# A transformer block on one core: projections two batches further ahead, reciprocals issued between the values' transfers

## The chip, the core and the metric

The kernel runs on one core of a Trainium2 chip. Five engines work side by side, each through its own list of instructions in order: TensorE (PE, matrix products; its weight loads are shown apart as PEld), VectorE (DVE), ScalarE (ACT), GpSimd (POOL) and SyncE (SP), which here issues nearly all transfers. They wait for one another through semaphores. Matmul results stand in PSUM, everything else on chip in SBUF. The metric is the device time of one launch in microseconds (us). An engine that is idle costs nothing unless the work that ends last waits for it.

## What is computed

A batch of 16 sequences, 256 positions of 256 features each, all in float32, goes through one block:

```
x = x + attention(layernorm(x))       # 16 heads of 16 features
x = x + ffn(layernorm(x))             # 256 -> 1024 -> 256
attention: softmax(q @ k.T / 4, keys up to 16 positions ahead) @ v, then @ wo.T
ffn:       silu(h @ gate.T) * (h @ up.T), then @ down.T
```

`gate`, `up` and `down` are not inputs. Each is 1024 x 256 values of a cubic (Catmull-Rom) interpolation of 2033 control points, so the kernel has to make the three matrices before the first feed-forward.

## The kernel before

**Tiling.** A batch is a tile of 128 partitions by 2 x 256. Q and K are kept transposed in `qks`, four heads to a group `g`, each head in its own 32 partitions: 16 features and, for the query, a row with the negated maximum of its scores, so that the exponent is the product itself. `vs` holds V with a column of ones, whose product is the softmax's denominator. Both are rings of NQK = 3 buffers; batch b uses number b % 3. A buffer's constant rows are set once by POOL (`scores_and_values`, L162).

**Steps.** A loop of B + 4 = 20 steps (L596) is a software pipeline. Step s works on five batches at once:

- `pb = s`: `project_qk` (L233: four matmuls each for q and k, two ACT copies into `qkc`, eight transfers into `qks`) and `project_v` (L257); ahead of them, for batch s + 1, `stats_a`, `norm_a` and `turn_a` (mean and variance, normalised rows, transposition through PE and an ACT copy `xnT`).
- `nb = s - 1`: scores for the maxima. `inner` (L318, four per step) and `outer` (L348, two) compute blocks of scores on PE; `find_max` reads them on DVE. `turn_max` (L382) transposes the maxima (`pm`), and four transfers put them into `qks`.
- `tb = s - 2`: the scores again, now with the maximum's row, the exponentials on ACT, their masking on POOL, and `values` for two groups (`po`, copied by ACT into `au`). Maxima and exponentials of one `inner` or `outer` share two PSUM tiles of scores, and the next block of scores waits until both have read.
- `ob = s - 3`: the other half of `values`, then `gather` (L412): four transfers of denominators (`den`) and eight of values, from `au` into `ac`. `invert` (L428) takes the reciprocal on DVE, writes it to memory (`rd`) and reads it back spread over the heads' features (`rb`, two transfers). `divide`, `project_o` (`py`), the sum with x, `stats_f`, `norm_f`, `turn_f` (`ptf`, copied into `x2T`) follow in the same step.
- `s - 4`: the feed-forward. `gate_up` (L471) part i makes 256 of the 1024 intermediate rows, `down` (L493) the output rows, half by half; `out` is stored when the second is done. Part 0 is made a step earlier: at the end of step s, for batch s - 3.

**What sets the order.** `InOrder` (L78) keeps each engine's instructions in program order; the tile framework sees to the waits and buffers. So the order of the calls in the loop (L596 to L635) is the order of work on each engine. Between the attention's pieces lie seven numbered gaps; `fill(s, gap)` (L567) puts the feed-forward of an older batch there, so that PE has work while DVE and ACT read the scores. In steps s >= B, where nothing is projected, the parts of `gate_up` and `down` stand one gap earlier.

Steps 0 to 3 have no feed-forward yet. There the table `heads` (L554) puts into a gap some splines, which make the three matrices (`spline`, L520: four matmuls `pw`, two ACT copies, two predicated DVE copies), and a number of unused products: `keep_running(n)` multiplies the identity with itself n times into a PSUM tile that nothing reads (`run`). Their number over all gaps is 67, after 12 ahead of the first step.

```
heads = {
    (0, 7): (0, 5),
    (1, 1): (1, 3), (1, 3): (1, 9), (1, 4): (0, 6), (1, 5): (1, 3), (1, 6): (0, 4), (1, 7): (0, 11),
    (2, 1): (1, 0), (2, 3): (1, 2), (2, 5): (1, 0), (2, 6): (0, 2), (2, 7): (0, 11),
    (3, 3): (0, 7), (3, 6): (0, 4),
}   # (step, gap): (splines, unused products)
```

**Buffers.** `xs`, the batches' rows, have nine buffers, since a batch's rows are needed from `stats_a` to the output. `au`, `inter`, `qkc` and `xnT` have two each. Two PSUM banks (`ps_m`) serve all products of the attention but the scores, in turn.

Of the kernel before, what the change touches and what calls it, by code (L numbers as in the profile page):

```python
# [11 lines left out]
F32 = mybir.dt.float32  # L12
# [6 lines left out]
P = 128  # L19
B, S, DIM = 16, 256, 256  # L20
H, HD = 16, 16
G = 4
# [71 lines left out]
def block_kernel(  # L94
# [13 lines left out]
    pe, dve, act, pool, sp = (  # L108
        InOrder(tc, e) for e in (nc.tensor, nc.vector, nc.scalar, nc.gpsimd, nc.sync)
    )  # L110
# [3 lines left out]
    sb1 = ctx.enter_context(tc.tile_pool(name="sb1", bufs=1))  # L114
    sb4 = ctx.enter_context(tc.tile_pool(name="sb4", bufs=4))
    sb6 = ctx.enter_context(tc.tile_pool(name="sb6", bufs=6))
    sbx = ctx.enter_context(tc.tile_pool(name="sbx", bufs=9))
    dr = ctx.enter_context(tc.tile_pool(name="dr", bufs=2, space=bass.MemoryType.DRAM))
    ps_s = ctx.enter_context(tc.tile_pool(name="ps_s", bufs=1, space=PSUM))
    ps_f = ctx.enter_context(tc.tile_pool(name="ps_f", bufs=2, space=PSUM))  # L120
# [5 lines left out]
    def load_x(b, engine):  # L126
        xs[b] = sbx.tile([P, 2, DIM], F32, tag="x", name=f"x{b}")
        engine.dma_start(xs[b], x[b].rearrange("(c p) d -> p c d", p=P))

    load_x(0, sp)  # L130
    w_in = {}
    for nm, src in (("q", wqT), ("k", wkT), ("v", wvT), ("o", woT)):
# [8 lines left out]
    for w in range(3):  # L141
        sp.dma_start(cp_in[:, w, :], cps[w])
        if w == 0:
            sp.dma_start(second_in, second)
    load_x(2, sp)


    ident = const.tile([P, P], F32, tag="ident", name="ident")
# [3 lines left out]
    mask0 = const.tile([P, JB], F32, tag="mask0", name="mask0")  # L152
    mask1 = const.tile([P, S], F32, tag="mask1", name="mask1")
    masks = (mask0, mask1)
    NQK = 3
    qks = [
        const.tile([P, 2, G, S], F32, tag=f"qk{i}", name=f"qk{i}") for i in range(NQK)
    ]
# [3 lines left out]
    def scores_and_values(i):  # L162


        pool.memset(qks[i][:, 1], -1.0)

        pool.memset(vs[i], 0.0)
        pool.memset(vs[i][:, :, :, HD : HD + 1], 1.0)
# [13 lines left out]


    xns, xnTs, mxs, aus, aos, recs, x2s, x2Ts = ({} for _ in range(8))
    es, inters, pgs = {}, {}, {}

    moments = {}

# [42 lines left out]
        transposed(xns.pop(b), xnTs[b], f"ta{b}")  # L231

    def project_qk(b):  # L233
        qkc = sb.tile([P, 2, 2, S], F32, tag="qkc", name=f"qkc{b}")
        for i, nm in enumerate("qk"):
            pq = ps_m.tile([P, 2, S], F32, tag="m", name=f"p{nm}{b}")
            for oc in range(2):
                for kc in range(2):
                    pe.matmul(
                        pq[:, oc, :],  # L240
                        lhsT=w_in[nm][:, kc, oc * P : (oc + 1) * P],
                        rhs=xnTs[b][:, kc, :],
                        start=(kc == 0),
                        stop=(kc == 1),
                    )
            act.activation(
                qkc[:, i], pq, AF.Copy, scale=HD**-0.5 if nm == "q" else 1.0
            )
        for gg in range(2):
            for r in range(4):  # L250
                at = 64 * gg + 16 * r

                (act if b == 0 and r % 2 else sp).dma_start(
                    qks[b % NQK][32 * r : 32 * r + HD, :, gg::2, :], qkc[at : at + HD]
                )
# [136 lines left out]

    def values(b, g2):
        if g2 == 0:
            aus[b] = sb.tile([P, G, S], F32, tag="au", name=f"au{b}")
        po = ps_m.tile([P, 2, S], F32, tag="m", name=f"po{b}_{g2}")
        for gg in range(2):
            g = 2 * g2 + gg
            for c, i, n in ((0, 0, S), (1, I1, W1)):
                for r in range(4):  # L400
                    pe.matmul(
                        po[32 * r : 32 * r + 32, gg, i : i + n],
                        lhsT=vs[b % NQK][:, c, 4 * g + r, :],
                        rhs=es[b, 1, g2, r // 2][:, r % 2, gg, :]
                        if c
                        else es[b, 0, g, r // 2][:, r % 2, :],
                        start=(c == 0),
                        stop=(c == 1),
                    )
        act.copy(aus[b][:, 2 * g2 : 2 * g2 + 2, :], po)  # L410

    def gather(b):  # L412

        au = aus.pop(b)
        den = sb.tile([4 * H, 64], F32, tag="den", name=f"den{b}")
        for g in range(G):
            sp.dma_start(
                den[16 * g : 16 * g + 16, :],
                au[HD:P:32, g, :].rearrange("r (q c) -> r q c", q=4),
            )  # L420
        recs[b] = den
        aos[b] = sb.tile([P, 2, S], F32, tag="ac", name=f"ac{b}")
        for gg in range(2):
            for r in range(4):
                at = 64 * gg + 16 * r
                sp.dma_start(aos[b][at : at + HD], au[32 * r : 32 * r + HD, gg::2, :])

    def invert(b):  # L428
        den = recs.pop(b)
        rec = sb.tile([4 * H, 64], F32, tag="rec", name=f"rec{b}")  # L430
        dve.reciprocal(rec, den)
        rd = dr.tile([H, S], F32, tag="rd", name=f"rd{b}")
        sp.dma_start(rd.rearrange("h (q c) -> (h q) c", q=4), rec)
        rb = sb.tile([P, 2, S], F32, tag="rb", name=f"rb{b}")
        for oc in range(2):
            sp.dma_start(
                rb[:, oc, :],
                rd[8 * oc : 8 * oc + 8, :].unsqueeze(1).to_broadcast([8, HD, S]),
            )
        recs[b] = rb  # L440
# [29 lines left out]

    def gate_up(b, i):  # L471
        if i == 0:
            inters[b] = sb.tile([P, 8, S], F32, tag="inter", name=f"inter{b}")
        pp = []
        for nm, w in (("g", gateT), ("u", upT)):
            t = ps_f.tile([P, 2, S], F32, tag="f", name=f"p{nm}{b}_{i}")
            for ic in range(2):
                for kc in range(2):
                    at = (2 * i + ic) * P
                    pe.matmul(  # L480
                        t[:, ic, :],
                        lhsT=w[:, kc, at : at + P],
                        rhs=x2Ts[b][:, kc, :],
                        start=(kc == 0),
                        stop=(kc == 1),
                    )
            pp.append(t)
        th = sb.tile([P, 2, S], F32, tag="th", name=f"th{b}_{i}")
        act.activation(th, pp[0], AF.Tanh, scale=0.5)
        dve.scalar_tensor_tensor(th, th, 1.0, pp[0], ALU.add, ALU.mult)  # L490
        dve.tensor_tensor(inters[b][:, 2 * i : 2 * i + 2, :], th, pp[1], ALU.mult)
# [21 lines left out]
    def coefficients(w):  # L513

        dve.scalar_tensor_tensor(
            cp_in[:, w, :], cp_in[:, w, :], 0.5 if w == 2 else 1.0, tab_in[:, 0:NPART],
            ALU.mult, ALU.mult,
        )
# [28 lines left out]
    def do(stage, b, *args):  # L547
        if 0 <= b < B:
            stage(b, *args)
# [2 lines left out]


    heads = {  # L554
        (0, 7): (0, 5),
        (1, 1): (1, 3), (1, 3): (1, 9), (1, 4): (0, 6), (1, 5): (1, 3), (1, 6): (0, 4), (1, 7): (0, 11),
        (2, 1): (1, 0), (2, 3): (1, 2), (2, 5): (1, 0), (2, 6): (0, 2), (2, 7): (0, 11),
        (3, 3): (0, 7), (3, 6): (0, 4),
    }
    parts = iter([(w, part) for part in range(2) for w in range(2)] + [(2, 0), (2, 1)])  # L560

# [5 lines left out]
    def fill(s, gap):  # L567

        n, idle = heads.get((s, gap), (0, 0))
        if idle:  # L570
            keep_running(idle)
        for _ in range(n):
            spline(*next(parts))

        late = s >= B
        for what, at in (
            ((gate_up, s - 4, 1), 1),
            ((gate_up, s - 4, 2), 2 if late else 3),
            ((gate_up, s - 4, 3), 3 if late else 4),
            ((down, s - 4, 0), 4 if late else 5),  # L580
            ((down, s - 4, 1), 5 if late else 6),
            ((gate_up, s - 3, 0), 7),
        ):
            if at == gap:
                do(*what)


    for t in tiles:
# [5 lines left out]
    norm_a(0)  # L594
    turn_a(0)
    for s in range(B + 4):  # L596
        pb, nb, tb, ob = s, s - 1, s - 2, s - 3
        if 3 <= s + 2 < B:
            load_x(s + 2, sp)
        inner(nb, tb, 0)  # L600
        do(values, ob, 1)
        do(gather, ob)
        if s == 1:
            coefficients(2)
        do(stats_a, pb + 1)
        if s == 0:
            for i in range(1, NQK):
                scores_and_values(i)
        fill(s, 1)
        do(norm_a, pb + 1)  # L610
        if s == 0:
            coefficients(0)
            coefficients(1)
        inner(nb, tb, 1)
        do(invert, ob)
        do(project_qk, pb)
        fill(s, 2)
        outer(nb, tb, 0)
        fill(s, 3)
        inner(nb, tb, 2)  # L620
        do(values, tb, 0)
        do(turn_a, pb + 1)
        do(divide, ob)
        fill(s, 4)
        inner(nb, tb, 3)
        do(project_o, ob)
        do(stats_f, ob)
        fill(s, 5)
        do(norm_f, ob)
        outer(nb, tb, 1)  # L630
        fill(s, 6)
        do(turn_f, ob)
        do(project_v, pb)
        do(turn_max, nb)
        fill(s, 7)  # L635


# [27 lines left out]
```

## Time and profile before

| what | value |
|---|---|
| median of three runs | 680.85 us (678.76 to 681.75) |
| the profiled execution | 683.28 us, its span 681.6 us |
| mean granted TensorE clock | 0.990 |
| PE, scores | 4096 matmuls, 106.4 us busy |
| PE, `pg`, `pu`, `pd` | 127.3, 121.5 and 117.0 us |
| PE, `run` | 158 matmuls, 22.1 us |
| DVE, maxima | 512 of 362 ns, and 512 reads of 83 ns |
| ACT, exponentials | 192 of 615 ns |
| transfers | 29.65 MB, 44 GB/s on average |

The profile comes from one execution, so sums against it are made with its own 681.6 us of span. The span runs from the first to the last instruction; 1.7 us of the execution lie around it. A float32 matmul appears as two records, so 79 unused products are 158 records; transposes appear as one. Where a row of the timeline merges several instructions, it gives the start of the first, the time from there to the end of the last, and how many; brackets hold the engine's idle time before it and what released it. "SPq" rows are transfers being issued, not carried. The ends of matmuls are modelled; the distance from the start of one group to the start of the next is the safer measure of what a group takes.

### The profile page before, as it was taken

The numbers are of one execution on the slowest core, as the hardware profiler recorded it, in microseconds if no ns is written. First come the engines' busy times: TensorE is split into PE (matmuls) and PEld (weight loads), VectorE is DVE, ScalarE is ACT, GpSimd is POOL, SyncE is SP. The second block draws the span as 40 slices with busy tenths as digits, with TensorE's granted clock in tenths as the row PEclk, the third lists the DMA queues.
The fourth block names the chain that finished last, engine by engine and source line by source line (L and its number), as shares of the span: only waits on it lengthen the run. The fifth ranks groups of instructions, "written<-read, shape, count | busy, mean of one in ns | idle before, by whom it ended". The sixth has DMA issues, their size and how long they took to land.

```text
span 681.6 us, 18745 instructions
## 1 busy us (share of the span) xinstructions
PE 661.8 (97%) x7534; PEld 520.9 (76%) x7534; DVE 358.0 (53%) x1473; ACT 230.0 (34%) x413; POOL 124.1 (18%) x244
## 2 busy tenths in 40 slices
PE   7999899999999999999999999999999999999998
PEld 6676677878777787877778787877778787676876
DVE  5656555465464546466454546556554546523332
ACT  2245434243333424243333424333342423232110
POOL 5012211122121212122111112211121111212000
PEclk9999989999999999999999999999999999999989
DMA  7302303021121313012121302112030301010100
GB/s 218 54 17 51 64 21 65 17 67 17 50 49 40 59 33 63 21 43 40 48 51 35 64 18 64 21 50 48 25 59 19 58 24 36 16 27 27 33 15 15
DMA packets 34422, 29.65 MB, mean 44 GB/s; under 512 B 7840, under 2 KB 33696, under 8 KB 34336
## 3 DMA queue, kind: packets, MB, share of 16 engines
q1 hardware_dynamic: 32928, 27.15, 18.0%
q10 hardware_dynamic: 1408, 1.31, 0.7%
q8 instruction: 59, 0.97, 0.6%
q14 instruction: 27, 0.22, 0.1%
HBM read 10.88 MB, written 4.46 MB: 23 GB/s over the span
## 4 chain that ended last, share of the span: by engine, by line
PE 87%; DVE 1%; ACT 0%; issue 0%; POOL 0%; DVEq 0%
PE pg L88 18%; PE pd L88 17%; PE pu L88 16%; PE scores L88 12%; PE po L88 7%; PE py L88 5%; PE pv L88 3%; PE pq L88 3%; PE pk L88 3%; PE ptf L88 1%; PE pta L88 1%; PE pm L88 1%; DVE z L88 0%; ACT e L88 0%; DVE x L88 0%
## 5 line engine op out<-in xcount | busy, mean ns | idle before, releaser
L88 ACT ACTIVATE e<-scores 128x512 f32<-128x512 f32 (+1 forms) x192 | 117.5, 615 | 266.2 <-PE scores L88 206.2
L88 DVE CUSTOM_DVE_ANT_0 z<-scores,mask 128x144 bf16<-128x144 f32 (+1 forms) x512 | 154.5, 362 | 73.8 <-ACT qkc L88 35.5
L88 POOL TENSOR_SCALAR_AFFINE_SELECT e<-e 128x224 f32<-128x224 f32 (+1 forms) x192 | 94.3, 492 | 448.4 <-ACT e L88 448.1
L88 PE MATMUL pg<-x2T,gateT 128*128 128x256 f32 x512 | 127.3, 392 | 1.4 <-ACT x2T L88 1.4
L88 PE MATMUL pu<-x2T,upT 128*128 128x256 f32 x512 | 121.5, 380 | 0.0
L88 DVE SCALAR_TENSOR_TENSOR th<-th,pg 128x512 f32<-128x512 f32 x64 | 44.0, 687 | 140.5 <-ACT th L88 140.5
L88 PE MATMUL pd<-downT,inter 128*128 128x256 f32 x512 | 117.0, 382 | 0.0
L88 PE MATMUL scores<-qk 17*64 17x144 f32 (+7 forms) x4096 | 106.4, 317 | 3.9 <-ACT e L88 1.8
L88 PEld LDWEIGHTS pg<-x2T,gateT 128*128 128x128 f32 x512 | 94.1, 193 | 19.0 <-DVE mx L88 3.1
L88 PEld LDWEIGHTS pu<-x2T,upT 128*128 128x128 f32 x512 | 97.9, 191 | 13.5
L88 PEld LDWEIGHTS pd<-downT,inter 128*128 128x128 f32 x512 | 96.1, 190 | 14.1 <-DVE mx L88 0.2
L88 PEld LDWEIGHTS scores<-qk 17*64 17x64 f32 (+1 forms) x4096 | 69.2, 131 | 40.0 <-issue 30.1
L88 ACT ACTIVATE th<-pg 128x512 f32<-128x512 f32 x64 | 38.2, 597 | 72.2 <-PE pg L88 72.0
L88 DVE TENSOR_TENSOR inter<-th,pu 128x512 f32<-128x512 f32 x64 | 44.0, 688 | 26.6 <-PE pu L88 26.6
L88 PE MATMUL po<-e,v 128*32 128x256 f32 (+1 forms) x1024 | 50.0, 336 | 0.0
L88 PEld LDWEIGHTS po<-e,v 128*32 128x32 f32 x1024 | 29.5, 109 | 23.3 <-issue 12.3
L88 DVE DVE_READ_ACCUMULATOR2_ANT mx<- 128x1 f32 x512 | 42.4, 83 | 0.1
L88 DVE TENSOR_TENSOR x<-x,pd 128x256 f32<-128x256 f32 x32 | 13.5, 421 | 51.5 <-PE pd L88 51.5
L88 PE MATMUL py<-wo,ac 128*128 128x256 f32 x128 | 33.3, 405 | 2.4 <-issue 2.4
L88 PE MATMUL pq<-xnT,wq 128*128 128x256 f32 x128 | 31.9, 392 | 1.1 <-ACT xnT L88 0.7
L88 PEld LDWEIGHTS py<-wo,ac 128*128 128x128 f32 x128 | 23.9, 196 | 11.0 <-issue 7.0
L88 PE MATMUL pv<-wv,xnT 128*128 128x256 f32 x128 | 31.5, 391 | 0.0
(54 smaller groups left out, 421.7 us busy)
## 6 DMA issues: line engine op xcount, KB each, us to landing
qk<-qkc SPq DMA_DIRECT2D x124, 64.0 KB
x<-x SPq DMA_DIRECT2D x16, 256.0 KB
ac<-au SPq DMA_DIRECT2D x128, 32.0 KB
rb<-rd SPq DMA_DIRECT2D x32, 128.0 KB
out<-x SPq DMA_DIRECT2D x15, 256.0 KB
qk<-mxT SPq DMA_DIRECT2D x64, 4.0 KB
den<-au SPq DMA_DIRECT2D x64, 4.0 KB
cp_in<-cps SPq DMA_DIRECT2D x3, 256.0 KB
```

What stands on the lines that cost most here:

```text
L88: return self.tc.keep_in_program_order(fn(*args, **kwargs))
```

## The change

Projections run two batches further ahead (`AHEAD = 2`). In step s from 4 on, batch s + 2 is projected, and batch s + 3 has its statistics, norm and transposition. The two batches that this takes are made up for in steps 1 to 3: a table `projections` says for steps 0 to 3 what is prepared or projected in which gap, and `heads` has other numbers of unused products and two splines in other gaps. Steps 14 and 15 project nothing.

The rings `qks` and `vs` get five buffers, x gets ten; `au` and `inter` get one each, where they had two. `project_qk` is cut in two: the products and copies, and `spread`, the eight transfers, which can come later. A batch's load comes four steps ahead, after `invert` in place of the step's start; the third load now comes before the table `second`, and a fourth after the control points.

Of the eight transfers of values, `gather` issues four; the other four follow the store of the reciprocals in `invert`. `norm_a` stands after `inner(1)` and `invert`, no longer ahead of them. In `fill`, the earlier places of `gate_up` now begin at step 14; those of `down` begin at step 17 (`alone`), no longer at 16.

```diff
-    sbx = ctx.enter_context(tc.tile_pool(name="sbx", bufs=9))
+    sbx = ctx.enter_context(tc.tile_pool(name="sbx", bufs=10))
...
+    AHEAD = 2
     load_x(0, sp)
...
         if w == 0:
+            load_x(2, sp)
             sp.dma_start(second_in, second)
-    load_x(2, sp)
+    load_x(3, sp)
...
-    NQK = 3
+    NQK = 3 + AHEAD
...
     def project_qk(b):
-        qkc = sb.tile([P, 2, 2, S], F32, tag="qkc", name=f"qkc{b}")
+        qkcs[b] = qkc = sb.tile([P, 2, 2, S], F32, tag="qkc", name=f"qkc{b}")
...
+    def spread(b):
+        qkc = qkcs.pop(b)
         for gg in range(2):
...
-            aus[b] = sb.tile([P, G, S], F32, tag="au", name=f"au{b}")
+            aus[b] = sb1.tile([P, G, S], F32, tag="au", name=f"au{b}")
...
-        for gg in range(2):
-            for r in range(4):
-                at = 64 * gg + 16 * r
-                sp.dma_start(aos[b][at : at + HD], au[32 * r : 32 * r + HD, gg::2, :])
+        gather_heads(b, 0)
+
+    def gather_heads(b, gg):
+        for r in range(4):
+            at = 64 * gg + 16 * r
+            sp.dma_start(aos[b][at : at + HD], aus[b][32 * r : 32 * r + HD, gg::2, :])
...
         sp.dma_start(rd.rearrange("h (q c) -> (h q) c", q=4), rec)
+        gather_heads(b, 1)
+        del aus[b]
...
-            inters[b] = sb.tile([P, 8, S], F32, tag="inter", name=f"inter{b}")
+            inters[b] = sb1.tile([P, 8, S], F32, tag="inter", name=f"inter{b}")
...
     heads = {
-        (0, 7): (0, 5),
-        (1, 1): (1, 3), (1, 3): (1, 9), (1, 4): (0, 6), (1, 5): (1, 3), (1, 6): (0, 4), (1, 7): (0, 11),
-        (2, 1): (1, 0), (2, 3): (1, 2), (2, 5): (1, 0), (2, 6): (0, 2), (2, 7): (0, 11),
-        (3, 3): (0, 7), (3, 6): (0, 4),
+        (0, 7): (0, 6),
+        (1, 1): (1, 0), (1, 4): (1, 2), (1, 5): (1, 2), (1, 6): (0, 5), (1, 7): (0, 5),
+        (2, 1): (1, 0), (2, 3): (1, 6), (2, 5): (1, 1), (2, 6): (0, 4),
+        (3, 3): (0, 5), (3, 6): (0, 6),
     }
...
-        late = s >= B
+        alone = s > B
+        late = s >= B - AHEAD
         for what, at in (
             ((gate_up, s - 4, 1), 1),
             ((gate_up, s - 4, 2), 2 if late else 3),
             ((gate_up, s - 4, 3), 3 if late else 4),
-            ((down, s - 4, 0), 4 if late else 5),
-            ((down, s - 4, 1), 5 if late else 6),
+            ((down, s - 4, 0), 4 if alone else 5),
+            ((down, s - 4, 1), 5 if alone else 6),
...
+    projections = {
+        (0, 1): ((stats_a, 1),),
+        (0, 2): (
+            (norm_a, 1), (coefficients, 0), (coefficients, 1), (stats_a, 2),
+            (scores_and_values, 1), (scores_and_values, 2), (project_qk, 0), (spread, 0),
+        ),
+        (0, 4): ((turn_a, 1), (norm_a, 2)),
+        (0, 6): ((project_v, 0),),
+        (1, 1): ((turn_a, 2), (coefficients, 2)),
+        (1, 2): ((project_qk, 1), (spread, 1)),
+        (1, 3): ((project_qk, 2), (spread, 2), (scores_and_values, 3)),
+        (1, 6): ((project_v, 1),),
+        (1, 7): ((stats_a, 3), (norm_a, 3), (project_v, 2)),
+        (2, 1): ((turn_a, 3), (stats_a, 4), (scores_and_values, 4)),
+        (2, 2): ((norm_a, 4), (project_qk, 3), (spread, 3)),
+        (2, 4): ((turn_a, 4),),
+        (2, 6): ((project_v, 3),),
+        (2, 7): ((stats_a, 5), (norm_a, 5), (project_qk, 4)),
+        (3, 1): ((turn_a, 5), (stats_a, 6)),
+        (3, 2): ((norm_a, 6), (spread, 4), (project_qk, 5), (spread, 5)),
+        (3, 3): ((project_v, 4),),
+        (3, 4): ((turn_a, 6),),
+        (3, 6): ((project_v, 5),),
+    }
+
+    def project(s, gap):
+        if s < 4:
+            todo = projections.get((s, gap), ())
+        else:
+            pb = s + AHEAD
+            todo = {
+                1: ((stats_a, pb + 1),),
+                2: ((norm_a, pb + 1), (project_qk, pb), (spread, pb)),
+                4: ((turn_a, pb + 1),),
+                6: ((project_v, pb),),
+            }.get(gap, ())
+        for stage, b in todo:
+            do(stage, b)
...
         inner(nb, tb, 1)
         do(invert, ob)
-        do(project_qk, pb)
+        if s + 2 + AHEAD < B:
+            load_x(s + 2 + AHEAD, sp)
+        project(s, 2)
         fill(s, 2)
...
         do(turn_f, ob)
-        do(project_v, pb)
+        project(s, 6)
         do(turn_max, nb)
+        project(s, 7)
         fill(s, 7)
```

`project(s, 1)` is called where `stats_a` was, `project(s, 4)` where `turn_a` was, and `project(s, 3)` after `outer(0)`, where no call stood.

## The prediction

> **What bounds the kernel now.** I read the busy shares first, then the clock row, then the span cut at the steps of the outer loop, and then the timeline where PE stands still.
>
> ```profile
> PE 661.8 (97%) x7534; PEld 520.9 (76%) x7534; DVE 358.0 (53%) x1473; ACT 230.0 (34%) x413; POOL 124.1 (18%) x244
> ...
> PEclk9999989999999999999999999999999999999989
> ```
>
> PE is the bound, nearly everywhere; DVE, the next, is half idle. The clock row has two dips, near 85 us and near the end. The second view gives each stretch's length and every engine's busy time in it, then granted clock and DMA. I cut at the first `scores` matmul of a step (97.42 opens step 4):
>
> ```profile
> 16.75:41.78 25.03, 23.35 (x254) 16.65 (x255) 15.72 (x78) 6.12 (x13) 0.69 (x1) 1.00 0.27 39
> 41.78:65.11 23.33, 21.44 (x374) 15.11 (x373) 15.12 (x77) 13.14 (x25) 6.28 (x13) 1.00 0.21 37
> 65.11:97.42 32.31, 27.62 (x402) 20.92 (x401) 16.24 (x82) 11.88 (x22) 6.95 (x14) 0.89 0.22 45
> 97.42:136.29 38.87, 38.87 (x460) 30.85 (x459) 21.44 (x91) 13.99 (x25) 7.36 (x14) 1.00 0.20 43
> ...
> 563.50:600.28 36.78, 35.14 (x431) 27.08 (x431) 19.70 (x84) 11.60 (x20) 6.66 (x13) 0.95 0.10 25
> ```
>
> Steps 1 to 3 are a ramp with PE idle 1.7, 1.9 and 4.7 us; in step 4 PE never stops, and steps 5 to 14 repeat its 38.87. Step 15, without `turn_a`, takes 38.48. Step 16, the last row, projects nothing (3.65 for q and k, 1.73 for v, by the timeline's row starts) and should take 38.48 - 5.38 = 33.10, but takes 36.78. So time saved on PE late counts in full only if steps don't stop as step 16 does. The ramp's worst place is the first `divide`:
>
> ```profile
> 69.54 5.16 SPq L88 DMA_DIRECT2D ac<-au  x8
> ...
> 74.81 1.18 SPq L88 DMA_DIRECT2D rd<-rec  x1
> ...
> 77.28 1.35 SPq L88 DMA_DIRECT2D rb<-rd  x2
> ...
> 81.78 0.69 DVE L88 TENSOR_TENSOR ac<-ac,rb 128x512 f32<-128x512 f32 x1 [2.89 <-DMA qk<-qkc]
> ...
> 82.57 3.46 PE L88 MATMUL py<-wo,ac 128*128 128x256 f32 x8 [2.35 <-issue]
> ...
> 89.83 1.13 PE L88 MATMUL ptf<-ident,xnf 128*128 128x128 f32 x4 [1.50 <-DVE xnf L88]
> ```
>
> SP issues eight value transfers, then `rd`, whose reciprocal had been ready since 72.64, then `rb`; `divide` starts 4.50 after `rb`. PE waits, and `py` runs 3.4 where it takes 1.83 in step 4: half clock.
>
> **Dummies and late projections.** (1) The listing of the changed program's instructions has 42 dummy matmuls of `run` in place of 67 (the opening 12 stay): 25 x 0.232 (eleven took 2.55) = -5.8 us of PE. Two batches' projections move from steps 14 and 15 into steps 1 to 3: 2 x (3.65 + 1.73 + 0.49 for `pta`) = 11.7 us. They take with them, per batch, 2.1 us of DVE statistics and norm, 2.5 of ACT copies and a power of 0.7 on POOL. Two more `qk`/`v` pairs cost POOL 2 x 2.1 us of memsets; POOL is 18% busy, and nothing reads those buffers before step 2.
>
> (2) **Start.** The fourth load, 256 KB, enters a DMA stretch that ends at about 11.4 us at 375 KB per us: +0.7, over before the first `qk` transfers at 13.12. `stats_a(2)` and `norm_a(2)`, 2.1 us, fit DVE's idle 13.7 to 18.47. The nearest bad row is `xna` at 9.50, which took 2.98 in place of 0.73 while POOL set memory; the same here would end at about 17.7. Bounds -0.5 to +0.8, taken 0.
>
> (3) **Step 1** gains `pq`, `pk` and `pv` of batch 2 (5.38) and loses 22 dummies, 5.1. Two splines now stand close, so the second waits for the first's DVE copies (half a microsecond): +0.7. SP issues eight more transfers, 31 to 36 us, before the `mxT` ones near 40.
>
> (4) **Step 2** gains `pta` 0.49 and `pq`/`pk` of batch 4 (3.65), and has 11 dummies in place of 15. Of its 1.9 us of waits some fill, but four more dummies ahead of the third spline delay `downT`'s copies and the DVE chain behind them by 1.1: +2.4 (bounds +1.2 and +3.2).
>
> (5) **Step 3** gains `pta` and `pv`, 2.2 us, with dummies 11 as before. On SP the load leaves the front (-0.44) and the reciprocal goes out after four transfers. DVE loses the norm (0.7) and a wait of 0.8 before the reciprocal, so `rd` leaves near +7.0 us of the step (before +9.7); four heads take 2.6 more and cover its landing (2.47 from `rd` to `rb`), and `rb` leaves at +10.7 (before +12.17): `divide` at +15.2, `py` possible at +16.0. PE, delayed by the new work, arrives at +15.9. So `py` moves from +17.46 to +16.0, runs 1.83 in place of 3.39, and `ptf` follows its end by the same 3.86 (add, statistics, power, norm). From there `ptf` 0.44, `pv` 1.73, `pm` 0.22, `pg` and `pu` 3.55 make a step of 27.7: -4.6. What is late next is that norm: 1.4 us of PE idle remain.
>
> **The clock there.** These rows are windows of 3.41 us, the length of each drop in the clock record; the first two stand directly before a drop to half, the third does not:
>
> ```profile
> 86.29:89.70 3.41, 2.03 (x72) 1.75 (x57) 2.46 (x8) 0.65 (x1) 1.28 (x2) 1.00 0.00 0
> 591.47:594.88 3.41, 1.77 (x70) 1.45 (x70) 2.98 (x19) 1.67 (x3) 0.93 (x2) 1.00 0.23 77
> ...
> 625.60:629.01 3.41, 2.37 (x41) 1.39 (x39) 1.07 (x3) 1.67 (x3) 1.39 (x3) 1.00 0.25 83
> ```
>
> PE busy for 2.03 lost the clock, 2.37 kept it. The Trainium skill, "TensorE: Matmul & The Clock Gate", section "Why this matters for your kernels", would have no gap over about 3 us, else half rate; by it the 1.4 us cost nothing. By the rows a window around 1.4 us of idle holds 2.0 busy and is lost: 3.41 at half, +1.7. I follow the rows. Taking dummies out is thus a risk only where under about 2.2 of 3.41 us remain busy. Ramp: 0 + 0.7 + 2.4 - 4.6 + 1.7 = **+0.2**.
>
> **Steady steps 4 to 12.** Same PE work: 0. The norm moves behind the reciprocal on DVE; its `turn_a` comes far later. `rb` now leaves behind four heads, at about +12.7 of the step in place of +11.9; `divide`, at +18.0, waits for the third inner `scores` anyway. `au` gets one buffer: ACT's copy of the next batch's first half must now wait for this batch's last value transfer. That copy is at +18.0; the transfer is issued by +12.7 and, allowing it even the 4.5 of `rb`, lands by +17.2. Beyond +18 the copy stops ACT, behind it `xnT` and the exponentials of `inner(3)`, and so PE, microsecond for microsecond. `inter` with one buffer costs nothing: `down` reads it on PE ahead of the next `pg`.
>
> **Tail.** Step 13 loses `pta`: -0.4. Step 14 loses `pta`, `pq`, `pk` and `pv`. But `pv` covered a copy:
>
> ```profile
> 519.09 0.60 PE L88 MATMUL ptf<-ident,xnf 128*128 128x128 f32 x4
> ...
> 519.52 1.89 PE L88 MATMUL pv<-wv,xnT 128*128 128x256 f32 x8
> 519.72 0.59 ACT L88 COPY x2T<-ptf 128x512 f32<-128x512 f32 x1 [2.12 <-PE ptf L88]
> ...
> 521.47 1.89 PE L88 MATMUL pg<-x2T,gateT 128*128 128x256 f32 x8
> ...
> 592.49 0.71 PE L88 MATMUL ptf<-ident,xnf 128*128 128x128 f32 x4
> ...
> 594.84 0.58 PE L88 MATMUL pm<-ident,mx 128*16 128x128 f32 x2 [1.64 <-DVE mx L88]
> 595.21 3.41 PE L88 MATMUL pg<-x2T,gateT 128*128 128x256 f32 x8
> ```
>
> With `pv`, 2.38 from `ptf` to `pg`. Without it, `pg` waits for `x2T`: 1.46 from `ptf` to `pg`, as in step 18 (654.23 to 655.69). So `pv` gives 0.92, not 1.73. Also the gap after the first half of the values has no filler left; DVE and ACT are done with `inner(2)` about 2.85 after its `scores`, PE after 0.97 + 1.49: 0.4 lost. Step 14: -0.4 - 3.65 - 0.9 + 0.4 = -4.6; step 15, with no `pta` to lose, -4.2.
>
> Step 16 stops because nothing stands between `outer(1)` and `ptf`: maxima and exponentials are unread (`pm` waits 1.64), and the clock drops. `alone = s > B` moves `down(1)`, 3.56 us, into that place. Then `ptf` to `pu`, 5.97 now, takes 1.46 + 1.73 = 3.19; with the 0.4: -2.4. Idle 0.8 leaves 2.6 of a window busy, above 2.37: clock kept. Steps 17 to 19 keep their order. Tail: -0.4 - 4.6 - 4.2 - 2.4 = **-11.6**.
>
> **Sum:** -11.4 on a span of 681.6: 670.2. Around it lie 1.7 us (the profiled execution took 683.28): 671.9. The three runs' median, 680.85, is 2.4 below that execution; taking the change off the median gives **669.5**.
>
> **Rivals.** (a) As summed, 0.60; own range 666 to 673, from the ramp's bounds and one clock drop more or less. (b) The ramp gives more back: `rb`, now followed by a load and two spreads, lands no earlier and the two drops stay. For it: the wait's releaser at 81.78 is named as `qk<-qkc`, so transfers overlap there; against: they stand behind `rb` in the queue. Step 3 then saves nothing: +3.1 in place of +0.2, 672.4; with another drop 674. Chance 0.20. (c) The late steps turn DVE-bound and stop as step 16 does now, 3.6 us each: step 14 -2.2, 15 -1.8, 16 nothing, 13 -0.4; with the ramp -4.2, so 676.6. Against: `down(1)` stands in between. Chance 0.12. (d) Slower: the single `au`. From a landing of the last value transfer at +18 each microsecond is paid in some 13 steps; it outweighs 11.4 at +18.9, and at +19.3 gives 669.5 + 16.9 = 686. For it: the four heads now wait in SP behind `rd`, so behind DVE; against: 5 us from issue are left. Chance 0.08. That the order isn't changed as described is excluded by the instruction listing.
>
> **Numbers.** A difference under 0.5%, 3.4 us, can't be told from none. Faster: (a), (b) and over half of (c), 0.87; same 0.05; slower 0.08. The range 664.5 to 676.5 leaves out (d), half of (c) and the low end of (a), under 0.2.
>
> **What would show it.** `py` of batch 0 waiting under 0.5 us at full clock; `rd` between two groups of four `ac`; steps 14 to 16 near 34.3; `ptf` to `pg` about 1.5 in them; no drop in step 16. Wrong if PE idles before `po`'s successors in steps 4 to 13, or if step 2 grows over 4 us.

## The result and the profile after

The changed kernel takes **673.49 us** (median of four runs, 670.90 to 675.17), the one before 680.45 beside it (678.76 to 681.75): ratio 0.990, 95% interval 0.986 to 0.994. The forecast was 669.5. Over all runs of this study the medians are 673.48 (12 runs) and 680.06 (121 runs).

The page of the changed kernel, busy shares and granted clock; its span is 669.2 us of an execution of 670.9:

```profile
PE 652.2 (97%) x7484; PEld 511.6 (76%) x7484; DVE 358.5 (54%) x1473; ACT 230.3 (34%) x413; POOL 128.1 (19%) x250
...
PEclk9999999999999999999999999999999999999999
```

PE is as full as before, 50 records fewer. Both dips of the clock row are gone in this execution. The view of stretches, cut at the same matmuls (first column the stretch, then its length, then PE, PEld, DVE, ACT and POOL, granted clock, DMA share, GB/s): steps 1, 2, 3, 4, 13, 14 and 16.

```profile
16.48:42.47 25.99, 24.70 (x234) 16.54 (x235) 16.46 (x79) 7.94 (x17) 4.30 (x7) 1.00 0.40 58
42.47:69.83 27.36, 25.84 (x386) 17.86 (x385) 17.21 (x84) 14.52 (x27) 8.91 (x17) 1.00 0.18 32
69.83:98.70 28.87, 26.57 (x414) 20.42 (x413) 16.10 (x82) 13.71 (x26) 7.08 (x14) 1.00 0.36 68
98.70:137.57 38.87, 38.87 (x459) 30.85 (x459) 21.46 (x91) 13.97 (x25) 7.43 (x14) 1.00 0.20 43
...
448.56:487.04 38.48, 38.48 (x456) 30.46 (x455) 19.74 (x84) 13.46 (x24) 6.69 (x13) 1.00 0.18 37
487.04:521.22 34.18, 33.44 (x432) 26.09 (x431) 19.70 (x84) 11.63 (x20) 6.64 (x13) 1.00 0.10 27
...
555.40:589.58 34.18, 33.44 (x432) 26.09 (x431) 19.79 (x84) 11.63 (x20) 6.65 (x13) 1.00 0.10 26
```

Against the same stretches of before:

| stretch | before | after | difference | forecast |
|---|---|---|---|---|
| start | 16.75 | 16.48 | -0.3 | 0 |
| step 1 | 25.03 | 25.99 | +1.0 | +0.7 |
| step 2 | 23.33 | 27.36 | **+4.0** | +2.4 |
| step 3 | 32.31 (clock 0.89) | 28.87 (1.00) | -3.4 | -4.6, and +1.7 for a clock drop |
| steps 4 to 12, each | 38.87 | 38.87 | 0 | 0 |
| step 13 | 38.87 | 38.48 | -0.4 | -0.4 |
| steps 14 and 15 | 38.87, 38.48 | 34.18, 34.18 | -9.0 | -8.8 |
| step 16 | 36.78 (0.95) | 34.18 (1.00) | -2.7 | -2.4 |
| step 17 to the end | 81.28 | 79.60 | -1.6 | 0 |

The differences sum to -12.4, one microsecond from the -11.4 forecast. Yet the medians differ by 7.0. The two executions are not typical: the record of before has four clock drops (at 82.9, 89.7, 594.9 and 656.3 us, each 3.41 us at half clock, 6.8 us lost), the record of after has none. So this pair of traces shows a clock difference which the medians don't. Below, "clock loss" is (1 - mean granted clock) x span, and a mean over a kernel's runs is given where it decides. "Time less clock loss" is the mean time less that mean.

### The profile page after: what moved, and what is told of

Same layout as the page of the kernel before. It is cut to its first block, busy times and chain, and to the rows that moved or that the text cites. A ratio compares the mean times of both kernels' runs of the same rounds, so it can differ in the third digit from the quotient of the medians.

```text
span 669.2 us, 18583 instructions
## 1 busy us (share of the span) xinstructions
PE 652.2 (97%) x7484; PEld 511.6 (76%) x7484; DVE 358.5 (54%) x1473; ACT 230.3 (34%) x413; POOL 128.1 (19%) x250
## 3 DMA queue, kind: packets, MB, share of 16 engines
q1 hardware_dynamic: 32928, 27.15, 18.1%
## 4 chain that ended last, share of the span: by engine, by line
PE 94%; ACT 2%; DVE 2%; DMA 1%; issue 1%; POOL 0%; SPq 0%; ACTq 0%; DVEq 0%
PE pg L88 18%; PE pd L88 17%; PE pu L88 17%; PE scores L88 14%; PE po L88 6%; PE pq L88 5%; PE py L88 5%; PE pk L88 4%; PE pv L88 4%; PE pta L88 1%; PE ptf L88 1%; PE run L88 1%; PE pw L88 1%; ACT e L88 1%; DMA qk<-qkc 1%
## 5 line engine op out<-in xcount | busy, mean ns | idle before, releaser
L88 PE MATMUL pg<-x2T,gateT 128*128 128x256 f32 x512 | 125.1, 387 | 2.8 <-ACT x2T L88 2.8
L88 PEld LDWEIGHTS pg<-x2T,gateT 128*128 128x128 f32 x512 | 92.3, 190 | 21.2 <-ACT x2T L88 4.2
L88 PEld LDWEIGHTS scores<-qk 17*64 17x64 f32 (+1 forms) x4096 | 68.6, 131 | 37.8 <-issue 29.2
L88 PEld LDWEIGHTS po<-e,v 128*32 128x32 f32 x1024 | 29.6, 109 | 23.3 <-issue 12.5
L88 PE MATMUL py<-wo,ac 128*128 128x256 f32 x128 | 31.8, 391 | 1.1 <-ACT e L88 1.1
```

The lines of the kernel that those rows point to most:

```text
L88: return self.tc.keep_in_program_order(fn(*args, **kwargs))
```

## The experiments

All times are medians; ratios are to the kernel before, run beside each.

### Both kernels again

Both unchanged.

> The kernel before, unchanged, to see each run's granted clock. Theory (the clock): the four drops to half clock of the profiled execution cost 6.8 us of its 683.28, so at full clock it takes about 676.5; each run is that plus 1.7 us for each drop of 3.41 us, and the median of 680.5 has two or three drops (clock 0.993 to 0.994). Rival (the profile tells the time): runs don't follow their clock, and spread by something else.

> The changed kernel, unchanged. Theory (the clock): its profiled execution of 670.9 had no drop and is the kernel's time at full clock; runs with a mean clock of 0.995 have two drops and take 670.9 + 3.4 = 674.3. The difference at full clock is then 676.5 - 670.9 = 5.6, and what the medians differ by beyond it is the number of drops. Rival: time and clock are not tied; the runs at 0.995 take 671 as well, or the slow ones have full clock.

| | runs | median | range | mean clock loss | runs at a clock of 0.999 or more |
|---|---|---|---|---|---|
| before, all runs | 121 | 680.06 | 676.4 to 684.6 | 4.41 (117 runs) | 676.4 to 677.3 (4 runs) |
| after, all runs | 12 | 673.48 | 669.8 to 677.1 | 2.52 | 669.8 to 671.1 (4 runs) |

The repeat of after gave 672.6, ratio 0.991 (0.987 to 0.994), its trace steps of 25.98, 27.36 and 28.98, then 34.18 three times: the lengths of the first trace. The repeat of before had one clock drop of 10.24 us at 81.2, and a step 16 of 35.20 at full clock (the first row below; the second is step 3 of `before_alone`, an experiment below that does not touch this step):

```profile
562.82:598.02 35.20, 33.56 (x432) 25.98 (x431) 19.71 (x84) 11.60 (x20) 6.64 (x13) 1.00 0.10 26
...
65.03:95.92 30.89, 25.96 (x401) 19.93 (x400) 16.24 (x82) 11.87 (x22) 6.92 (x14) 0.94 0.23 47
```

At full clock the kernels stand at about 677.1 and 670.7 (medians of four runs each): **-6.4**. In the medians the clock brings 0.2 more. The mean clock losses differ by 1.9, so it brings less than 2 in any case, not the 6.8 of the first pair of traces. Before's runs follow the clock: 678.4 at 0.997 (16 runs), 680.0 at 0.995 (42), 682.7 at 0.987 (9). In these 117 runs a microsecond of clock loss goes with 0.73 us of time, in after's 12 with about 1.1, so taking off the whole loss is a rough measure.

### The unused products

`after_no_idle` leaves them out in `fill` (42; the opening 12 stay):

```diff
-        if idle:
+        if False:
```

`after_fill` has more of them, where PE stands still; in `heads`:

```diff
-        (1, 1): (1, 0), (1, 4): (1, 2), (1, 5): (1, 2), (1, 6): (0, 5), (1, 7): (0, 5),
+        (1, 1): (1, 2), (1, 4): (1, 2), (1, 5): (1, 2), (1, 6): (0, 5), (1, 7): (0, 5),
...
-        (3, 3): (0, 5), (3, 6): (0, 6),
+        (3, 3): (0, 5), (3, 6): (0, 10),
+        (14, 7): (0, 2), (15, 7): (0, 2), (16, 7): (0, 2), (17, 7): (0, 2),
+        (18, 6): (0, 3), (18, 7): (0, 2),
```

> The changed kernel with the 42 unused products of steps 0 to 3 left out (the 12 at the start stay); the output is the same. Theory (they are mostly paid on PE): 42 x 0.232 = 9.7 us leave PE, of which about half stood beside waits; at full clock about 5 us less, 666, but PE windows under 2.2 us of 3.41 in the ramp lose the clock two or three times more, 3.4 to 5 us, so about the same, 673 plus or minus 2. Rival (they are free fillers): no time at full clock is gained and the extra drops cost, 677 or more. Second rival (clock doesn't mind): 668 or less.

> The changed kernel with 19 more unused products, each group shorter than the PE wait it stands in: two ahead of step 1's first spline, four more ahead of step 3's ptf, two ahead of pg in steps 14 to 17, and in step 18 three ahead of ptf and two ahead of pg. Theory (the clock): no step gets longer at full clock, so time minus clock loss stays at 670.2 to 670.6 within 0.4, and the drops in step 3, at the end of step 18 and in step 1 get rarer: mean loss under 1.5 us in place of 2.4, median 671 to 672. Rival (PE pays for each product): 19 x 0.23 = 4.4 us more, 675 or above at equal clock.

Steps 1 to 3 without the unused products, stretches as above:

```profile
16.75:42.56 25.81, 24.38 (x206) 15.20 (x207) 16.57 (x79) 7.33 (x15) 4.29 (x7) 0.87 0.40 58
42.56:70.40 27.84, 24.62 (x364) 16.23 (x363) 17.23 (x84) 15.08 (x29) 8.91 (x17) 0.94 0.18 32
70.40:99.08 28.68, 25.63 (x391) 18.95 (x391) 16.21 (x82) 13.72 (x26) 7.02 (x14) 0.94 0.37 68
```

PE has 22 to 28 records fewer in each step, yet the steps are no shorter; the clock column says why. It fell in all three. The median is 672.84, ratio 0.990 (0.986 to 0.994), as after's own. Its runs lost 7.62 us to the clock in the mean, 5.1 more than after's; the time less that loss is 665.2, where after has 670.6; with only 0.73 us taken off for each microsecond lost, as in before's runs, the two are 667.3 and 671.3. So the unused products cost 4 to 5 us and save about as much, as expected.

More of them gave 672.05, 0.986 (0.983 to 0.989). Time less clock loss is 670.6, after's own, so they cost nothing where they stand. The clock loss is 1.88, not under 1.5 as expected; the traced execution still dropped once, at 88.1, in step 3 (31.44 long). Against after the gain is not clear.

### Step 2

`after_turn3` moves `turn_a(3)` from step 2 to the end of step 1, which has two unused products fewer for it:

```diff
-        (1, 1): (1, 0), (1, 4): (1, 2), (1, 5): (1, 2), (1, 6): (0, 5), (1, 7): (0, 5),
+        (1, 1): (1, 0), (1, 4): (1, 2), (1, 5): (1, 2), (1, 6): (0, 5), (1, 7): (0, 3),
...
-        (1, 7): ((stats_a, 3), (norm_a, 3), (project_v, 2)),
-        (2, 1): ((turn_a, 3), (stats_a, 4), (scores_and_values, 4)),
+        (1, 7): ((stats_a, 3), (norm_a, 3), (project_v, 2), (turn_a, 3)),
+        (2, 1): ((stats_a, 4), (scores_and_values, 4)),
```

`after_less23` instead has four unused products fewer in gap (2, 3), as few as before has there. The spline behind them is step 2's second, the first of the two for `down`; the prediction and the expectation call it the third:

```diff
-        (2, 1): (1, 0), (2, 3): (1, 6), (2, 5): (1, 1), (2, 6): (0, 4),
+        (2, 1): (1, 0), (2, 3): (1, 2), (2, 5): (1, 1), (2, 6): (0, 4),
```

> The changed kernel, with turn_a(3) at the end of step 1 in place of two of the five unused products there, no longer ahead of the spline in step 2. In step 2 of the changed kernel's trace the spline's last product waits for the ACT copy of xnT, and its four products take 2.7 us where 1.2 are needed. Theory: that wait goes, step 2 is 1 to 2 us shorter, step 1 the same within 0.3. Rival: DVE, which reads the scores and then copies upT, sets the next stage anyway: step 2 shorter by under 0.5 us.

> The changed kernel with two unused products in place of six ahead of step 2's third spline. Theory of the prediction: the four delay the spline, its copies to downT and the DVE work behind them, so step 2 is 0.9 to 1.1 us shorter without them. Rival (they stand in a wait): step 2 shorter by under 0.3 us, and the clock drops more often.

The timeline at the start of step 2, first of after, then with `turn_a` moved (start, length, engine, tiles; brackets hold the idle time before and what ended it):

```profile
44.03 1.13 PE L88 MATMUL pw<-cp_in,tab_in 32*128 32x512 f32 x6
45.03 0.58 ACT L88 COPY xnT<-pta 128x512 f32<-128x512 f32 x1
45.50 1.09 ACT L88 COPY upT<-pw 128x512 f32<-128x512 f32 x2
...
45.67 1.12 PE L88 MATMUL pw<-cp_in,tab_in 32*128 32x512 f32 x2 [0.51 <-ACT xnT L88]
46.72 1.04 PE L88 MATMUL scores<-qk 16*64 16x208 f32 x32
```

```profile
43.81 1.14 PE L88 MATMUL pw<-cp_in,tab_in 32*128 32x512 f32 x8
45.41 1.07 ACT L88 COPY upT<-pw 128x512 f32<-128x512 f32 x2
45.61 1.16 PE L88 MATMUL scores<-qk 16*64 16x208 f32 x32 [0.66 <-ACT e L88]
```

In after the new `pta` stands ahead of a spline. It lies in one of the two PSUM banks `ps_m`, and the kernel's code gives the spline's last two products both of them. So the last product waits until ACT has copied `pta` away (`xnT`), which ACT does only after an exponential, and the next scores start at 46.72. Without it the eight `pw` records run through and the scores start at 45.61. Step 2 is **25.99 instead of 27.36** (-1.37), step 1 unchanged (25.98). The median is 670.33, 0.987 (0.984 to 0.989); time less clock loss 669.4, against 670.6. The four unused products count for little: step 2 took 28.66 with a clock drop of 3.41 in it. A drop costs at most half its length, 1.7, so without it the step takes at least 26.95, and the four cost at most 0.4. The kernel took 674.77, 0.992 (0.990 to 0.995), and 670.6 less clock loss, as after.

### The reciprocal and the first division

`after_rd_late` puts all eight value transfers ahead of `rd`; `before_rd` is the kernel before with four of them behind it, as in the change:

```diff
     def gather(b):
...
         gather_heads(b, 0)
+        gather_heads(b, 1)
...
     def invert(b):
...
-        gather_heads(b, 1)
```

`after_load_late` and `after_spread_late` hold back step 3's load, the latter the spreads too, to a place after `stats_f`; the diff is that of the latter, and the former lacks its lines on spreads:

```diff
-        (3, 2): ((norm_a, 6), (spread, 4), (project_qk, 5), (spread, 5)),
+        (3, 2): ((norm_a, 6), (project_qk, 5)),
...
-        if s + 2 + AHEAD < B:
+        if s + 2 + AHEAD < B and s != 3:
             load_x(s + 2 + AHEAD, sp)
...
         do(stats_f, ob)
+        if s == 3:
+            load_x(s + 2 + AHEAD, sp)
+            spread(4)
+            spread(5)
```

> The changed kernel with all eight transfers of values ahead of the store of the reciprocals, as before the change. Theory: only step 3 feels it. rd leaves near +10 us of step 3 in place of +7.2, rb near +12.3 in place of +10.8, divide about 1.5 us later, so 1.5 us more and a second long PE wait ahead of py, with a clock drop more often: +1.5 to +3.2, 675 to 677. Rival (rb is bound by the load and the spreads behind it, not by when it leaves): under 0.5 us.

> The kernel before with the reciprocals' part of the change alone: rd is issued between the two groups of four transfers of values. Theory, from the two orders in the changed kernel (rd 3.65 us earlier brought divide 0.4 us): rd near +7.5 in place of +9.7 of step 3, divide earlier by 0.3 to 0.5, the wait ahead of py still 2 us and the clock still lost: under 0.5 us in the median, no difference that can be measured. Rival (the prediction's sum: divide follows rb by 4.5 and rb leaves 1.5 us earlier): divide near +15.2, py near +16, 1.5 us less and fewer drops, median under 678.

> The changed kernel with the load of step 3 alone issued behind project_o; the two spreads stay directly behind rb. It tells apart what holds rb back in step 3. If it is the load's 256 KB: divide about 4.1 us after rb, at +15.2 of step 3, as with load and spreads moved. If it is the spreads: divide stays 5 us or more behind rb, at +16.2 or later.

> The changed kernel with the load and the two spreads of step 3 issued only after project_o, behind divide; nothing else moves. In the changed kernel divide starts 5.0 to 5.4 us after rb is issued, in the kernel before 4.4 to 4.5. Theory (the load's 256 KB and the spreads share the engines with rb's 256 KB): divide comes 3.8 to 4.2 after rb, about 1.2 us earlier, the wait ahead of py (1.1 to 1.2) is gone, and step 3 is 1 us shorter. Rival (rb's own time): divide stays 5 us behind rb, no change.

After's timeline in step 3, SP's issues and what waits for them:

```profile
76.99 0.53 SPq L88 DMA_DIRECT2D rd<-rec  x1
77.56 2.96 SPq L88 DMA_DIRECT2D ac<-au  x4
80.62 1.33 SPq L88 DMA_DIRECT2D rb<-rd  x2
82.01 0.43 SPq L88 DMA_DIRECT2D x<-x  x1
82.49 12.02 SPq L88 DMA_DIRECT2D qk<-qkc  x16
86.02 0.69 DVE L88 TENSOR_TENSOR ac<-ac,rb 128x512 f32<-128x512 f32 x1 [1.65 <-DMA qk<-qkc]
86.81 1.97 PE L88 MATMUL py<-wo,ac 128*128 128x256 f32 x8 [1.12 <-ACT e L88]
```

`rd` and `rb` leave at +7.16 and +10.79 of the step, as forecast (+7.0, +10.7), but `divide` starts 5.40 after `rb`, and PE waits 1.12 us. The traces also keep the times at which parts of a transfer signal that they have landed, which the views above don't print. Each of the two `rb` transfers has one signal about 1.06 us after its issue and then eight more. In the table, the last three columns count from the issue of the first `rb`; the signals are those of the second:

| execution | load right behind `rb` | `rb` issued, from the step's start | sixth of the eight signals | last signal | `divide` |
|---|---|---|---|---|---|
| before (three traces), before_rd | no | +12.1 to +12.7, +11.57 | 3.56 to 3.95 | 4.11 to 4.37 | 4.43 to 4.66 |
| after_load_late | no | +11.33 | 3.58 | 4.11 | 4.33 |
| after, its repeat | yes | +10.79, +11.30 | 4.17, 3.64 | 5.18, 4.78 | 5.40, 5.00 |
| after_spread_late | yes | +11.04 | 3.77 | 3.93 | 4.15 |
| after_turn3, after_less23, after_fill | yes | +10.94 to +11.19 | 3.52 to 3.54 | 5.75 to 5.82 | 5.97 to 6.04 |
| after_rd_late, after_no_idle, combined | yes | +12.61, +10.34, +11.04 | 3.77, 3.44, 3.50 | 3.83, 3.58, 3.62 | 4.05, 3.80, 3.84 |

In all fourteen traces the first `rb` is complete 2.7 to 2.9 us after its issue, and `divide` follows the last signal of the second by 0.22 us (by 0.31 or 0.32 in the three of before). So `divide` waits for `rb` itself, and for its last part: the sixth signal differs by 0.7 us between the traces, the last by 2.2. In `after_turn3` the load behind `rb` sends its first signal at 3.78, two microseconds before the last of `rb` at 5.77: what stands behind in the queue need not land behind. The releaser that the row at 86.02 names, `qk<-qkc`, only uses a semaphore that an earlier `ac` transfer used too.

The row of `after_spread_late` is the one to look at. Its edit moved nothing: SP had nothing else to issue between `invert` and `stats_f`, so `x` and the spreads still follow `rb` at once, and SP's 641 entries stand in the same order in both traces. Its timeline:

```profile
84.42 1.32 SPq L88 DMA_DIRECT2D rb<-rd  x2
85.80 0.43 SPq L88 DMA_DIRECT2D x<-x  x1
...
88.56 0.69 DVE L88 TENSOR_TENSOR ac<-ac,rb 128x512 f32<-128x512 f32 x1 [0.65 <-DMA x<-x]
```

It is thus a third execution of after, and the three took 5.40, 5.00 and 4.15. With no load behind `rb` five traces lie within 0.33 us; with it nine lie between 3.8 and 6.0, with a mean of 4.9. That the load makes the last part's landing uncertain is what these rows suggest; a fixed price for it they don't show. `after_load_late` took 671.89, 0.988 (0.986 to 0.990), 669.8 less clock loss, 0.8 below after, which six runs don't settle. Why one part comes late in one execution and not in another stays **open**. `after_spread_late` as a repeat also tells how far medians of one program stray: 674.84 (six runs, clock loss 3.93) against 673.48; less the loss 670.7 and 670.6.

What the order of the transfers is worth hangs on that landing. Undone, the changed kernel takes 674.21, 0.991 (0.989 to 0.994). `rd` leaves 3.65 us later, but its trace had no late part, and `divide` is only 0.36 to 0.47 later than in the first two traces of after; it is 1.5 later than in the third, which had none either. The time less clock loss is 671.2 against 670.6, no clear difference. Done in before alone, `divide` starts 0.5 to 0.9 us earlier, and the kernel takes 678.79, 0.998 (0.996 to 1.000), against 680.35 beside it. At full clock three runs of it took 675.4 to 676.0, where before's four took 676.4 to 677.3. With 0.73 us taken off for each microsecond lost it stands 0.6 below before. So the order is worth some 0.6 to 1.5 us there, between the expectation (under 0.5) and its rival (1.5).

### Step 16 alone

`down` in the kernel before moves to the later gap at step 16, as in the change.

```diff
-            ((down, s - 4, 0), 4 if late else 5),
-            ((down, s - 4, 1), 5 if late else 6),
+            ((down, s - 4, 0), 4 if s > B else 5),
+            ((down, s - 4, 1), 5 if s > B else 6),
```

> The kernel before, with one part of the change: in step 16 down keeps its later gaps, so that down(1) stands between outer(1) and ptf. Theory: step 16 goes from 35.2 (at full clock; 36.8 with the drop) to about 33.1 + 0.8 + 0.4 = 34.2, and the drop in it is gone: 1 us less at full clock, 1 to 2 us less in the median (678 to 679). Rival (step 16 is shortened only by what the projections leave): under 0.3 us.

Its timeline in step 16:

```profile
591.26 0.60 PE L88 MATMUL ptf<-ident,xnf 128*128 128x128 f32 x4
591.69 0.38 PE L88 MATMUL pm<-ident,mx 128*16 128x128 f32 x2
592.53 1.99 PE L88 MATMUL pg<-x2T,gateT 128*128 128x256 f32 x8 [0.46 <-ACT x2T L88]
```

`pm` no longer waits for the maxima and `pg` starts 1.27 after `ptf`. Step 16 takes 34.18, against 35.20 at full clock and 36.78 with a drop. One microsecond is below what the medians resolve here: 680.89, 1.001 (0.999 to 1.002). Its 14 runs lost more to the clock (5.24 us in the mean); with 0.73 us taken off for each microsecond lost they stand 0.8 below before.

### A version that beats both

`after_turn3` and `after_fill` together. The edit of `after_spread_late` is also in it and, as there, moves nothing on any engine.

> The changed kernel with those fillers, turn_a(3) in step 1, and the load and spreads of step 3 behind divide. Theory: the parts add where they stand, step 2 -1.4 and step 3 -1.1, so 668.1 at full clock, and with few drops a median of 668 to 670, 0.3 to 0.6% under the changed kernel. Rival (what step 2 or step 3 gains is given back in the next wait, or the phase of the clock's windows decides): median 671 or above.

Its steps 1 to 3:

```profile
16.69:42.99 26.30, 24.77 (x239) 16.97 (x239) 16.45 (x79) 8.25 (x18) 4.30 (x7) 1.00 0.39 57
42.99:68.98 25.99, 24.31 (x381) 17.30 (x380) 17.11 (x84) 14.11 (x27) 8.94 (x17) 1.00 0.19 34
68.98:96.70 27.72, 27.44 (x421) 21.34 (x421) 16.19 (x82) 13.71 (x26) 7.02 (x14) 1.00 0.39 71
```

**669.49 us** (668.90 to 670.06), ratio 0.982 (0.979 to 0.984): below the interval of after. The runs of before beside it stood at 682.1, two above the others', so that the ratio flatters it; by its own time it is 4.0 below after. Step 4 starts at 96.70, 2.0 earlier than after's. All five runs kept a clock of 0.999 or more. PE has no gap ahead of `py`: `divide` came 3.84 after `rb`, since no part of `rb` was late in this execution, and four more products of `run` filled the wait ahead of `ptf`. Less clock loss it stands at 669.2, 1.4 below after: the 1.37 of step 2. Most of the rest of its lead over after, 2.6 us, is clock: its runs lost 0.27 in the mean, after's 2.52.

## Why the forecast was right, and where it was off

The direction, the place and most sizes were right; the gain at full clock was 6.4 us where the forecast, freed of its clock terms, said 8.0, and the clock brought 0.2 in the medians where it said 3.4. Point by point:

- **Tail (-11.6).** Right. In step 14 `pg` follows `ptf` by 1.28 (forecast 1.46) and the scores after the first half of the values wait 0.28 us (forecast 0.4):

```profile
505.31 1.05 PE L88 MATMUL scores<-qk 16*64 16x208 f32 x32 [0.28 <-ACT e L88]
...
516.29 0.60 PE L88 MATMUL ptf<-ident,xnf 128*128 128x128 f32 x4
516.73 0.38 PE L88 MATMUL pm<-ident,mx 128*16 128x128 f32 x2
516.93 0.59 ACT L88 COPY x2T<-ptf 128x512 f32<-128x512 f32 x1 [2.17 <-PE ptf L88]
517.57 1.99 PE L88 MATMUL pg<-x2T,gateT 128*128 128x256 f32 x8 [0.46 <-ACT x2T L88]
```

  The late steps took 34.18 for a forecast of 34.3. That `pv` had covered a copy held: taking it out shortened the way from `ptf` to `pg` by 1.10 of its 1.73 (forecast 0.92). Of step 16's gain 1.0 is order, as `before_alone` shows, and the rest clock. At full clock the tail won 10.4.
- **Steady steps (0).** Right: in step 4 the last value transfer leaves at +12.5 and has landed by +14.5, and `au`'s copy is at +18.1. Rival (d), the single `au`, did not occur. Nor did (c): `down(1)` stands between `outer(1)` and `ptf`, and no late step stops.
- **Steps 1 and 2 (+0.7, +2.4).** Step 1 gave back 1.0. Step 2 gave back 4.03, over its bound of 3.2 and over the 4 us that the prediction named as a sign of being wrong: **the step of the forecast that failed in kind**. It charged the new `pta` by its 0.49 us of PE, where `pta`, by the bank it holds until ACT has copied it, cost 1.37. It charged the four unused products by a delay of 1.1, where they cost at most 0.4. And its terms make 0.49 + 3.65 - 0.93 + 1.1 = 4.3, so that +2.4 let all 1.9 us of PE's waits fill; PE's idle time in the step went from 1.89 to 1.52 only (23.33 - 21.44 and 27.36 - 25.84).
- **Step 3 (-4.6).** It took 28.87, forecast 27.7. The order of issues came as said, the landing did not (5.40 for 4.50), so `py` waited 1.12 us where the sign said under 0.5. Rival (b) is right in part: `rd` left 2.5 us earlier than in before's trace, and `divide` came 0.5 earlier. Its reason, the load and spreads behind `rb`, is not shown to be the cause. The prediction held against it that they stand behind `rb` in the queue; the signals show that this is no protection. It also read `qk<-qkc` as the releaser, which was not what `divide` waited for. The drops of before's trace went. No trace of before's step 3 is at full clock; the nearest, `before_alone` with one drop, took 30.89, so between 29.2 and 30.9 without it, and step 3 won 0.3 to 2.0 where the forecast, freed of its clock terms, has 1.2.
- **The clock (-3.4 in the sum).** The term that was mis-sized most. The drops of one execution were counted as won, 3.4 in step 3 and 1.7 in step 16, one drop (1.7) was put back, and the sum was then taken off a median of other executions. The medians differ by 0.2 for the clock, the mean losses by 1.9.

Together: -11.4 + 1.6 (at full clock) + 3.2 (clock) = -6.6, the difference of the medians over all runs. Of the 1.6 at full clock, step 2 is as much alone; step 1 adds 0.3, the start and the tail give back 0.8, and the balance leaves some 0.5 for step 3. So 673.5 lies where (b) put it, 672.4 to 674, outside the likeliest case's own 666 to 673, but mostly for other reasons than (b)'s: step 2 gave more back, and the clock gave less than was counted.

- **The rule on idle.** The step weighed a rule of the Trainium skill ("TensorE: Matmul & The Clock Gate", section "Why this matters for your kernels"), no gap over about 3 us, against two windows with 2.03 and 2.37 us busy of 3.41. That gaps well under 3 us can lose the clock was right: `after_turn3`, `after_less23` and `after_fill` waited 2.08, 1.84 and 2.15 us ahead of `py`, and the clock dropped at 86.5, 89.6 and 88.1, while after's 1.12 kept it. But `before_alone` waited 2.46 there and kept it: its gap lay across two windows, 2.24 and 2.13 us busy, where `after_turn3`'s lay in one, 1.60 busy. The windows with these gaps, two of `before_alone`, then that of `after_turn3`:

```profile
77.92:81.34 3.42, 2.24 (x53) 1.26 (x44) 0.91 (x6) 2.16 (x4) 1.13 (x3) 1.00 0.46 116
81.34:84.75 3.41, 2.13 (x28) 1.68 (x36) 2.20 (x10) 0.60 (x1) 0.39 (x2) 1.00 0.68 97
...
83.11:86.52 3.41, 1.60 (x40) 0.98 (x36) 0.79 (x3) 1.86 (x4) 0.76 (x2) 1.00 0.73 154
```

  A sharp threshold between 2.03 and 2.37 was wrong, as the last section shows.

## What to carry to other kernels

Before the clock drops of a profiled execution are counted as won, read the granted clock of many executions of both kernels; a difference at full clock and a difference in clock loss are two numbers. Price a moved piece of PE work by the bank it holds until its copy is done and by what waits for that bank, not by its own length. Don't count PE's waits as room for more work without asking what each of them waits for. An earlier issue is worth something only if the last part of the transfer lands earlier. Before a moved call is blamed or praised, see whether the order on its queue changed at all.

## What the runs showed of the hardware

- **The busy time of one window does not settle whether the clock is lost.** I cut the 14 traces into windows of 3.41 us, in step with their drops, and took the whole windows from 6 us on. Where PE was busy under 1.7 us, the next window was at half clock in all six cases; from 1.7 to 2.15 in nine of 21; from 2.15 to 2.7 in three of 41, all around the start of step 1; from 2.7 to 3.1 in four of 107, all in the ramp. In one place, the end of step 18, the four windows with 1.81 busy lost it and the eight with 1.87 to 2.09 kept it; in step 16 one with 1.77 lost it and one with 1.78 kept it. What else decides these runs don't show. Drops last 3.41 us or a multiple.
- **The same program's time wanders with this.** Before ranges from 676.4 to 684.6 us over 121 runs; in the 117 with a clock on record, a microsecond of clock loss goes with 0.73 us. The combined version, whose traced ramp has no long gap, stayed within 1.2 us in five runs.
- **A small read-back can take a third longer in one execution than in another, by its last part alone.** `rb`, two transfers of 128 KB, took 4.15 to 5.40 us from issue to use in three executions of one order of instructions. Over all fourteen traces six of the eight signals of its second transfer came within 4.2 us of the issue, the last between 3.6 and 5.8.
